# Row taps and group-norm moments placed at the slots in which ACT makes the silu

## The chip, the cores and the metric

The kernel runs on one core of a Trainium2 chip. The metric is the device time of one execution in microseconds. A core has five engines with a queue each: PE (TensorE, matmuls), DVE (VectorE), ACT (ScalarE), POOL (GpSimd) and SP (SyncE, which issues most of the transfers). An engine works through its own queue in order and waits for others by semaphores, so the time depends on where each instruction stands in its queue as much as on how many there are.

## The reference, cut to what matters

Four layers are applied to four images of 384 channels and 48 x 48 positions, each as `x = x + layer(groupnorm(x))`. Everything is float32.

```python
# layer 0: a selective state space model over the 2304 positions of an image
xin, z = split(norm(x) @ in_proj)
xin = silu(conv4(xin) + b)                       # 768 channels
dt, B, C = split(xin @ x_proj);  dt = softplus(dt @ dt_proj + b)
h[t] = exp(dt[t] * A) * h[t-1] + dt[t] * B[t] * xin[t]        # 768 channels x 16 states
y[t] = sum over states of h[t] * C[t]
out = layernorm(((y + xin * D) * silu(z)) @ out_proj)
# layer 1: 1x1 product, 8x8 patches filtered in the frequency domain, then
t = depthwise_conv3x3(t)                         # nine taps per channel
out = (gelu(t[:192]) * t[192:]) @ w_out
# layer 2: depthwise 11x11 convolution with kernels made from four points
# layer 3: four experts (384 -> 384 -> 384) weighted by a top-2 softmax gate
```

The group norm takes mean and variance of 12 channels over a whole image, so an image's layer can't begin before the moments of all its positions are known. For layer 0 these are moments of the input `x` itself.

## The kernel before, in words

**The scans.** Layer 0 sets the beat. An image is cut into five chunks of 460 or 464 positions. For each chunk there are 96 *slots*: 6 groups of 128 channels times 16 states, one state of one group per slot. There are 4 x 5 x 96 = 1920 slots, numbered through, and the number of the current one is kept in `place[0]`. In a slot `u` the function `scans` writes, in this order: background steps that begin on ACT; the scan of `u` on DVE (line 850); the other background steps; the product with C of `u` on DVE (line 870), or for the "slow" units one slot later on POOL (line 879); the decay `exp(dt * A)` of a later unit on ACT (line 826, three slots ahead in image 0, two ahead after it); the driving term of unit `u + 3` on POOL (line 837). After a scan and its product, ACT copies the last column to `carry` (line 864). PE sums the 16 states by transposing each result into PSUM (line 770).

**The background.** All other work is written as tasks: Python generators that yield an engine's name ahead of each step. A `Lane` holds a queue of tasks and in each slot moves each active task by at most one step, if the step's ring of buffers has room and its extra condition, the fourth entry of what is yielded, holds. A step on PE carries a weight, and the `Meter` admits no more of them into a slot when the sum is over a limit. Three lanes are served: `aux` with the rest of layer 0 (`plan` gives each task the slot of the chunk from which it may start), `one` with layers 1, 2 and the scores of the previous image, and `two` with its experts. The order of all instructions is thus fixed when the program is built. From slot 42 of images 1 to 3 the previous image's layers are put into `one` and `two`.

**The silu.** Once per chunk, `gates` takes the silu of the next chunk's `xc` and of this chunk's `zs`, 128 x 2760 elements each, on ACT (lines 693 and 696). Silu is in another table set than exp and ln, so a table load stands in front and one behind (line 548). It is due at slot 64 of a chunk and is written in slot 65.

**The moments of the next image.** `image_stats` loads half of 128 channels of the next image (1152 positions, three pieces of 384) into a buffer with the tag `on`, which the output of layer 0's projection also uses, lets six slots pass, and takes the moments of the three pieces on DVE (line 573), one piece per slot. It runs in the first three chunks of images 0 to 2, with the first half due at slot 43 and the second at 66.

**The taps.** `finish_strip` makes the nine taps of layer 1's 3 x 3 convolution for a strip of eight rows on DVE (lines 1272 and 1274), three channel groups in turn with one PSUM bank for the sum. A step takes three taps in two of four slots (`slow_slot`) and two in the others.

Of the kernel before, what the change touches and what calls it, by code (L numbers as in the profile page):

```python
# [133 lines left out]
def wait(slots):  # L134
    for _ in range(slots):
        yield ("pool",)
# [3 lines left out]
def tile_layers(ctx: ExitStack, tc: tile.TileContext, a: dict, out: bass.AP):  # L140
# [272 lines left out]
    with ExitStack() as first:  # L413
# [58 lines left out]
        with (  # L472
# [4 lines left out]
            for ct in range(CT):  # L477
                t = pp.tile([P, HW], F32, name=f"x0_{ct}")
# [62 lines left out]
        stats3 = [wp.tile([P, CT, len(BANDS), 6], F32, name=f"stats3_{b}") for b in range(2)]  # L541
        edges = [sum(BANDS[:k]) for k in range(len(BANDS) + 1)]

        ordered = [False]

        def table_back():

            ins = nc.scalar.preload_act_table_set("natural_log_exp_and_others")
            if not ordered[0]:
                tc.keep_in_program_order(ins)  # L550
# [2 lines left out]
            for _ in steps:  # L553
                pass

        def scans(wk, mm, ring, meter, place, lanes, begin):

# [6 lines left out]
            def image_stats(b, ct, h):  # L566
                t = wk.tile([P, TT * C], F32, name=f"xs0_{b}_{ct}_{h}", tag="on", bufs=1)
                half = HW // 2
                nc.sync.dma_start(t[:, :half], a["x"][b, bass.ts(ct, P), bass.ts(h, half)])
                yield from wait(6)  # L570
                for k in range(3):
                    yield ("dve",)
                    nc.vector.bn_stats(stats0[:, b % 2, ct, h, k, :], t[:, bass.ts(k, LB)])

            def image_norm(b):
# [112 lines left out]
            def gates(i, j):  # L688

                yield ("act",)  # L690
                if i is not None:
                    c, n = st[i], CHUNKS[G[i][1]]
                    nc.scalar.activation(c["xc"][:, :, :n], c["xc"][:, :, :n], AF.Silu)
                if j is not None:
                    c, n = st[j], CHUNKS[G[j][1]]
                    nc.scalar.activation(c["zs"][:, :, :n], c["zs"][:, :, :n], AF.Silu)
                table_back()
# [197 lines left out]
            def gate(i, m):  # L895
                (b, t), c = G[i], st[i]
                n = CHUNKS[t]
                w = n // TT
                yield ("pe", 0.45, (ring, 1))
                ps, r = ring.take(f"pyb{b}_{t}_{m}")  # L900
                for k in range(TT):
                    nc.tensor.transpose(
                        ps[:, bass.ts(k, w)], c["yt", m][:w, bass.ts(k, P)], ident[:w, :w]
                    )
                yield ("dve",)
                zm = c["zs"][:, m, :n]
                nc.vector.tensor_tensor(zm, ps[:, :n], zm, ALU.mult)
                ring.done(r)
# [75 lines left out]
            def plan(i, at):  # L984

                todo = []

                def put(q, name, make, *needs):
                    task = Task(make, [named[k] for k in needs if k in named], at + q)
                    named[name] = task  # L990
                    todo.append((q, task))

                more = i + 1 if i + 1 < len(G) else None
                if i:
                    for h in range(2):
                        put(6 + h, ("gate", i - 1, MT - 2 + h),
                            lambda h=h: gate(i - 1, MT - 2 + h))
                    for k in range(TT):
                        put(8 + 5 * k, ("out", i - 1, k), lambda k=k: out_proj(i - 1, k),
                            *[("gate", i - 1, m) for m in range(MT)])  # L1000
                    put(28, ("norm", i - 1), lambda: layer_norm(i - 1),
                        *[("out", i - 1, k) for k in range(TT)])
                    for ct in range(CT):
                        put(33 + 2 * ct, ("res", i - 1, ct), lambda ct=ct: residual(i - 1, ct),
                            ("norm", i - 1))
                if i < len(G):
                    b, t = G[i]
                    rest = [("res", i - 1, ct) for ct in range(CT)]
                    for j in range(MT):
                        put(30 + 4 * j, ("z", i, j), lambda j=j: project_z(i, j),  # L1010
                            ("out", i - 1, TT - 1), ("fold", b, 1))
                    for p in range(1, MT // 2):
                        put(PAIR * p - 12, ("steps", i, p), lambda p=p: steps(i, p))
                    for p in range(MT // 2):
                        put(PAIR * p + 14, ("skip", i, p), lambda p=p: skip(i, p))
                    done = [("z", i, j) for j in range(MT)]
                    if more is not None:
                        put(40, ("load", more), lambda: load(more), *rest)
                        for j in range(MT):
                            put(45 + 3 * j, ("x", more, j), lambda j=j: project(more, j),  # L1020
                                ("load", more), ("fold", G[more][0], 0))
                            done.append(("x", more, j))
                    put(64, ("silu", i), lambda: gates(more, i), *done)
                    if more is not None:
                        put(66, ("expand", more), lambda: expand(more), ("silu", i),
                            *[("steps", i, p) for p in range(MT // 2)])
                        put(82, ("steps", more, 0), lambda: steps(more, 0), ("expand", more))
                    for m, q in ((0, 67), (1, 69), (2, 74), (3, 76)):
                        put(q, ("gate", i, m), lambda m=m: gate(i, m), ("silu", i))
                    if b + 1 < NB:  # L1030
                        if t < CT:
                            put(43, ("stats", b, t, 0), lambda: image_stats(b + 1, t, 0), *rest)
                            put(66, ("stats", b, t, 1), lambda: image_stats(b + 1, t, 1),
                                ("stats", b, t, 0))
                        if t == CT:
                            put(48, ("mean", b + 1), lambda: image_norm(b + 1))
                            put(70, ("fold", b + 1, 0), lambda: fold(b + 1, 0),
                                ("mean", b + 1), *done)
                        if t == CT + 1:
                            put(54, ("fold", b + 1, 1), lambda: fold(b + 1, 1), *done[:MT])  # L1040
                aux.queue.extend(task for _, task in sorted(todo, key=lambda x: x[0]))
# [81 lines left out]

        def slow_slot():
            return place[0] % 4 < 2

        def later(b, ring, accr):

# [123 lines left out]
            def finish_strip(hb):  # L1252
# [7 lines left out]
                def taps(ct):  # L1260
                    yield ("dve", 0, (accr, 1))
                    acc, k = sums[ct] = accr.take(f"dw{b}_{hb}_{ct}")
                    v = acc[:, :LB].rearrange("p (h w) -> p h w", w=W)
                    room = 3 if slow_slot() else 2
                    for k in range(9):
                        if not room:
                            yield ("dve",)
                            room = 3 if slow_slot() else 2
                        room -= 1
                        src = d["pad", hb][:, ct, k // 3 : k // 3 + 8, k % 3 : k % 3 + W]  # L1270
                        if k == 0:
                            nc.vector.tensor_scalar_mul(v, src, w_dw[:, ct, 0:1])
                        else:
                            nc.vector.scalar_tensor_tensor(  # L1274
                                v, src, w_dw[:, ct, k : k + 1], v, ALU.mult, ALU.add
                            )
# [476 lines left out]

        rings = {}
        holder = [None]
        place = [0]

        def of_experts(pool, sizes):
            for tag, n in sizes.items():
# [16 lines left out]
        ring, accr = psum("mm", 3), psum("acc", 1)  # L1776
        meter = Meter(2.3, 2.0)
        one, two = Lane(8, meter), Lane(4, meter)
# [14 lines left out]
        with (  # L1793
            tc.tile_pool(name="l0", bufs=2) as wk,
            tc.tile_pool(name="l0p", bufs=2, space=PSUM) as mm,
        ):
            holder[0] = mm
            scans(wk, mm, ring, meter, place, [one, two], begin)
            held, two.queue = two.queue, []
            at = place[0]  # L1800
            while not all(ring.read):
                at += 1
                for act in (True, False):
                    two.step(act, at)
            two.queue = held
# [138 lines left out]
```

## Time and profile before

| | |
|---|---|
| median of three runs | 5437.34 us (5428.49 to 5438.78) |
| the profiled execution, its own time | 5425.31 us |
| its span, first to last instruction | 5423.4 us |
| mean granted TensorE clock | 0.913 |
| scan, line 850 | 1920 times, 1.16 to 1.18 us |
| decay, line 826 | 1920 times, 0.65 us |
| driving term, line 837 | 1920 times, 1.17 us |
| product with C on DVE, line 870 | 1035 times, 0.63 us |
| tap, line 1274 | 576 times, 0.61 us |
| moments of the next image, line 573 | 54 times, 0.53 us |
| silu, lines 693 and 696 | 20 each, 2.50 and 2.49 us |
| table load | 1.28 us |

The profile names an instruction by its engine, its line and its tiles, written as out<-in. A matmul of float32 stands twice in the trace, so a product of nine matmuls is 18 records. An instruction's recorded time runs a little into the next one's, so the distance of starts is often a better measure of what it costs than its own duration. Where an engine was idle, the profile gives the time and the instruction that ended it.

### The profile page before, as it was taken

What the parts mean: (1) busy time and instruction counts of PE and PEld (TensorE: products, weight loads), DVE (VectorE), ACT (ScalarE), POOL (GpSimd) and SP (SyncE); (2) the same over time, 40 slices, a digit from 0 to 9 for tenths busy, and PEclk for the clock granted to TensorE, in tenths of its full rate; (3) what the DMA queues carried; (4) which work ended last, traced back from release to release, by engine and by line L of the source; (5) the groups of instructions that cost most, each with busy time, mean ns of one, the idle gap of its engine ahead of it and who ended that gap; (6) DMA issues with size and microseconds to landing.
All of it is one profiled execution on the core that took longest, in us unless ns stands there. A gap on an engine that the chain in (4) does not pass through costs nothing. (4 is left out here: it accounts for less than half of the span.)

```text
span 5423.4 us, 81753 instructions
## 1 busy us (share of the span) xinstructions
PE 4666.9 (86%) x27796; PEld 3676.0 (68%) x27796; DVE 4053.8 (75%) x5581; ACT 2985.2 (55%) x6632; POOL 3365.2 (62%) x3020
## 2 busy tenths in 40 slices
PE   5677677687678988988789999988899999999899
PEld 4444454454347767665678887765678878889799
DVE  5999989889998788899887778899977674452200
ACT  3565565565558765655467655665566653334321
POOL 3878878876678788765667678775777673000000
PEclk8788788788789999999899999999999999999899
DMA  4445445454345555644566566554655554543200
GB/s 123 138 136 148 127 128 146 126 150 132 106 129 150 146 161 164 177 143 139 155 169 176 149 170 171 156 158 129 170 157 169 157 167 143 166 140 112 64 27 23
DMA packets 628391, 758.95 MB, mean 140 GB/s; under 512 B 58869, under 2 KB 622181, under 8 KB 627582
## 3 DMA queue, kind: packets, MB, share of 16 engines
q1 hardware_dynamic: 617668, 751.98, 48.2%
q8 instruction: 221, 3.62, 0.3%
q10 hardware_dynamic: 10298, 1.67, 0.2%
q14 instruction: 204, 1.67, 0.1%
HBM read 663.81 MB, written 89.65 MB: 139 GB/s over the span
## 5 line engine op out<-in xcount | busy, mean ns | idle before, releaser
L837 POOL TENSOR_TENSOR bu<-u,B 128x460 f32<-128x460 f32 (+1 forms) x1920 | 2227.5, 1170 | 778.2 <-DVE g L850 395.5
L826 ACT ACTIVATE da<-dt,a_neg 128x460 f32<-128x460 f32 (+1 forms) x1920 | 1242.8, 649 | 281.9 <-DVE g L870 185.4
L770 PE MATMUL y<-ident,g 128*115 128x128 f32 (+1 forms) x7680 | 1140.2, 297 | 274.1 <-DVE g L870 164.1
L770 PEld LDWEIGHTS y<-ident,g 128*115 128x115 f32 (+1 forms) x7680 | 1011.0, 187 | 502.3 <-DVE g L870 199.2
L879 POOL TENSOR_TENSOR g<-g,C 128x460 f32<-128x460 f32 (+1 forms) x885 | 1030.5, 1164 | 276.8 <-ACT carry L864 270.4
L850 DVE TENSOR_TENSOR_SCAN da<-da,carry,bu 128x460 f32<-128x460 f32 (+1 forms) x828 | 971.3, 1173 | 133.3 <-ACT da L826 94.7
L850 DVE TENSOR_TENSOR_SCAN g<-da,carry,bu 128x460 f32<-128x460 f32 (+1 forms) x708 | 819.7, 1167 | 83.5 <-ACT da L826 35.3
L870 DVE TENSOR_TENSOR g<-da,C 128x460 f32<-128x460 f32 (+1 forms) x1035 | 653.9, 632 | 91.7 <-PE y L770 31.5
L864 ACT COPY carry<-da 128x1 f32<-128x1 f32 x828 | 130.5, 158 | 824.3 <-DVE g L870 821.2
L1609 PE MATMUL pout<-hr,we 128*128 128x144 f32 x3456 | 483.6, 296 | 41.7 <-ACT hr L1625 31.7
L1609 PEld LDWEIGHTS pout<-hr,we 128*128 128x128 f32 x3456 | 455.4, 196 | 64.9 <-ACT hr L1625 42.6
L1609 PE MATMUL ph<-xe,we 128*128 128x144 f32 x3456 | 470.1, 291 | 13.4 <-DMA xe<-x3d 7.5
L1609 PEld LDWEIGHTS ph<-xe,we 128*128 128x128 f32 x3456 | 446.8, 194 | 30.6 <-issue 7.6
L1416 PE MATMUL pc<-band,row 128*128 128x162 f32 (+14 forms) x3456 | 458.8, 287 | 6.3 <-ACT row L1403 6.0
L1416 PEld LDWEIGHTS pc<-band,row 128*128 128x128 f32 x3456 | 446.2, 196 | 11.9 <-ACT row L1403 7.5
L1274 DVE SCALAR_TENSOR_TENSOR dw<-pad,w_dw,dw 128x384 f32<-128x384 f32 x576 | 347.6, 614 | 17.6 <-ACT pad L1249 6.7
L642 PE MATMUL pin<-xch,w_inx 128*128 128x463 f32 (+2 forms) x720 | 327.9, 595 | 34.7 <-DMA xch<-in_x 15.2
L921 PE MATMUL po<-w_out,zs 128*115 128x384 f32 (+1 forms) x960 | 341.5, 499 | 6.9 <-DVE dt L750 6.4
L1625 ACT ACTIVATE hr<-ph,nb 128x144 f32<-128x144 f32 x576 | 176.4, 377 | 305.2 <-PE ph L1609 303.6
L674 PE MATMUL pinz<-xch,w_inz 128*128 128x460 f32 (+1 forms) x720 | 316.8, 578 | 0.0
L1383 ACT ACTIVATE rep<-x,br,wr 128x192 f32<-128x192 f32 x576 | 274.3, 541 | 4.2 <-issue 4.2
L661 DVE SCALAR_TENSOR_TENSOR xc<-pin,conv_w,xc 128x460 f32<-128x460 f32 (+1 forms) x360 | 249.2, 692 | 30.9 <-ACT xc L655 19.2
(202 smaller groups left out, 5797.6 us busy)
## 6 DMA issues: line engine op xcount, KB each, us to landing
B<-bcd SPq DMA_DIRECT2D x768, 230.0 KB, 3.5
C<-bcd SPq DMA_DIRECT2D x768, 230.0 KB, 3.7
B<-bcd SPq DMA_DIRECT2D x192, 232.0 KB, 3.7
C<-bcd SPq DMA_DIRECT2D x192, 232.0 KB, 4.2
xe<-x3d SPq DMA_DIRECT2D x192, 216.0 KB, 2.8
ye<-y3d SPq DMA_DIRECT2D x144, 216.0 KB, 2.8
y3d<-ye SPq DMA_DIRECT2D x96, 216.0 KB, 2.2
xs<-x1d SPq DMA_DIRECT2D x24, 576.0 KB, 4.6
```

The source lines that it names most:

```text
L642: nc.tensor.matmul(ps[:, lo : halo + n], lhsT=w_inx[:, k, bass.ts(j, P)], rhs=c["x"][:, k, lo : halo + n], start=k == 0, stop=k == CT - 1,)
L674: nc.tensor.matmul(ps[:, :n], lhsT=w_inz[:, k, bass.ts(j, P)], rhs=c["x"][:, k, DCONV - 1 : DCONV - 1 + n], start=k == 0, stop=k == CT - 1,)
L770: nc.tensor.matmul(c["y", m][:w, bass.ts(k, P)], lhsT=src[:, bass.ts(k, w)], rhs=ident, is_transpose=True, start=c["terms", m] == 1 and k ...
L826: nc.scalar.activation(da[:, :n], c["dt", p][:, m % 2, :n], AF.Exp, scale=a_neg[:, m, s : s + 1])
L837: nc.gpsimd.tensor_mul(bu[:, :n], c["u", p][:, m % 2, :n], live["B", u // 2][:, :n])
L850: nc.vector.tensor_tensor_scan(here[:, :n], da[:, :n], bu[:, :n], last if t else nil[:, 0:1], ALU.mult, ALU.add,)
L870: nc.vector.tensor_mul(live["g", u][:, :n], live["h", u][:, :n], live["C", u // 2][:, :n])
L879: nc.gpsimd.tensor_mul(g[:, :n], g[:, :n], live["C", u // 2][:, :n])
L921: nc.tensor.matmul(ps[:w, :C], lhsT=c["zs"][:, m, bass.ts(k, w)], rhs=w_out0[:, m, :], start=m == 0, stop=m == MT - 1,)
L1274: nc.vector.scalar_tensor_tensor(v, src, w_dw[:, ct, k : k + 1], v, ALU.mult, ALU.add)
L1416: nc.tensor.matmul(d["acc2"][0][:, : BANDS[k] * W].rearrange("p (h w) -> p h w", w=W)[:, lo - edges[k] : hi - edges[k], xlo:xhi], lhsT=d[" ...
L1609: nc.tensor.matmul(ps[:, bass.ts(m, EB)], lhsT=w[:, k, bass.ts(m, P)], rhs=of[:, k, :], start=k == 0, stop=k == CT - 1,)
```

## The change

A function `gated` is true in the slot in which `gates` wrote its silus and in the next. The second half of `image_stats` waits until it is true and then takes its three moments in one slot; its load is due at slot 56 of the chunk instead of 66. A step of taps takes up to six while `gated` is true. `place`, so far handed to `scans`, is defined ahead of it. Nothing is added to or taken from the computation.

```diff
+        place = [0]
+        gated_at = [-9]
+
+        def gated():
+
+            return gated_at[0] <= place[0] <= gated_at[0] + 1
...
-        def scans(wk, mm, ring, meter, place, lanes, begin):
+        def scans(wk, mm, ring, meter, lanes, begin):
...
                 yield from wait(6)
+                if h:
+                    yield ("dve", 0, None, lambda: gated())
                 for k in range(3):
-                    yield ("dve",)
+                    if not h:
+                        yield ("dve",)
                     nc.vector.bn_stats(stats0[:, b % 2, ct, h, k, :], t[:, bass.ts(k, LB)])
...
                 yield ("act",)
+                gated_at[0] = place[0]
                 if i is not None:
...
-                            put(66, ("stats", b, t, 1), lambda: image_stats(b + 1, t, 1),
+                            put(56, ("stats", b, t, 1), lambda: image_stats(b + 1, t, 1),
                                 ("stats", b, t, 0))
...
+        def room_for_taps():
+            return 6 if gated() else 3 if slow_slot() else 2
+
...
-                    room = 3 if slow_slot() else 2
+                    room = room_for_taps()
                     for k in range(9):
                         if not room:
                             yield ("dve",)
-                            room = 3 if slow_slot() else 2
+                            room = room_for_taps()
```

More of the change, by code (lines that the diff above doesn't have):

```diff
@@ L1755, in tile_layers @@
         holder = [None]
-        place = [0]
         def of_experts(pool, sizes):
@@ L1797, in tile_layers @@
             holder[0] = mm
-            scans(wk, mm, ring, meter, place, [one, two], begin)
+            scans(wk, mm, ring, meter, [one, two], begin)
             held, two.queue = two.queue, []
```

## The prediction

> **What bounds the kernel now.** I read the shares by engine first, then who waited for whom, then the order of time around one silu, and last the busy time of stretches.
>
> ```profile
> PE 4666.9 (86%) x27796; PEld 3676.0 (68%) x27796; DVE 4053.8 (75%) x5581; ACT 2985.2 (55%) x6632; POOL 3365.2 (62%) x3020
> ```
> No engine bounds the whole. The 1920 scans (one per slot) run from 87 to 4525 us of the span, the rest of layers 1 to 3 after them. Busy time in stretches of 100 us has DVE at 88 to 96% and PE at 65 to 77% while image 0 is scanned, and PE at 90 to 100% where layers 2 and 3 run beside the scans. The chain that ended last is almost all PE, in the tail after 4525 us; the change leaves the order there as it was, so what it does to the scans shifts the end.
>
> Waits (microseconds in total, times, longest):
> ```profile
> POOL g L879 <- ACT carry L864: 270.4, 158, 8.2
> DVE da L850 <- ACT da L826: 107.3, 79, 8.1
> ```
> The silu slots make most of the second and part of the first. ACT around the first of them, in order of time (start, duration):
> ```profile
> 205.48 1.28 ACT L693 ACT_TABLE_LOAD   x1
> 206.77 2.50 ACT L693 ACTIVATE xc<-xc 128x2760 f32<-128x2760 f32 x1
> 209.18 2.49 ACT L696 ACTIVATE zs<-zs 128x2760 f32<-128x2760 f32 x1
> 211.68 1.28 ACT L548 ACT_TABLE_LOAD   x1
> ```
> ACT is shut for 7.5 us. DVE has three decays in hand, runs dry and waits:
> ```profile
> 208.22 1.17 DVE L850 TENSOR_TENSOR_SCAN g<-da,nil,bu 128x460 f32<-128x460 f32 x1
> 213.92 1.18 DVE L850 TENSOR_TENSOR_SCAN da<-da,nil,bu 128x460 f32<-128x460 f32 x1 [4.53 <-ACT carry L864]
> 216.92 0.64 DVE L907 TENSOR_TENSOR zs<-pyb,zs 128x460 f32<-128x460 f32 x1 [1.82 <-PE pyb L902]
> 223.28 1.17 DVE L850 TENSOR_TENSOR_SCAN da<-da,nil,bu 128x460 f32<-128x460 f32 x1
> 224.36 0.53 DVE L573 BATCH_NORM_STATS2 stats<-xs 128x6 f32<-128x384 f32 x1
> 224.81 0.62 DVE L870 TENSOR_TENSOR g<-da,C 128x460 f32<-128x460 f32 x1
> ```
> The 4.53 us are bubble, while three moments, the first at 224.36, stand in full slots soon after. In layer 1's stretches taps fill part of the hole already (silu slots 641, 1121, 1601):
> ```profile
> 1407.58 1.18 DVE L850 TENSOR_TENSOR_SCAN da<-da,carry,bu 128x460 f32<-128x460 f32 x1 [1.60 <-ACT carry L864]
> 2546.12 1.18 DVE L850 TENSOR_TENSOR_SCAN da<-da,carry,bu 128x460 f32<-128x460 f32 x1 [2.12 <-ACT da L826]
> 3747.91 1.18 DVE L850 TENSOR_TENSOR_SCAN da<-da,carry,bu 128x460 f32<-128x460 f32 x1 [4.75 <-ACT da L826]
> ```
>
> [...] the tiny carry copies behind the silus wait, and POOL's product behind a copy waits 7.04 us. [...] the silu starts 0.01 us after the load ends. [...] a moment is recorded with 0.53 us, but the product starts 0.45 us after it. I use such start-to-start times. [...]
>
> **The change, part by part.** The instructions are the same in number on every engine; only places move. I compared the two programs' orders, counting slots by scans. The silu slots are the same.
>
> *Second-half moments.* Nine groups of three (three chunks each before images 1 to 3) move from seven to nine slots after the silu into the silu slot, ahead of the bubble. Their load goes to SP's queue ten slots earlier (56 instead of 66). It needs the first half's moments, done five slots before, and the shared buffer "on" is next written at about slot 8 of the next chunk; neither waits. Inside the bubble a group takes 3 x 0.45 = 1.36 us of 4.53, so it is covered. Where it stood it cost less than 1.36: in a slot with a product on DVE the scan-to-product start distance is 1.26 us without a moment (1.08 to the moment), so a moment's removal saves 0.45 - 0.18 = 0.27; in a slot without, 0.45. Per group 0.27 + 0.45 + 0.27 = 1.0. The same slots of chunk 3 of image 0, which have no moments, take 1.8, 1.1, 1.8 us against 2.1, 1.5, 2.1: again 1.0.
> - Image 0 (silu slots 65, 161, 257): DVE bound, gaps of about 15 us in a chunk of 185: 3 x 1.0 = 3.0.
> - Slots 545, 737, 1025, 1217: the hole is 5.2 to 6.2 us, so cover is ample; but in the last three waits for PE follow within ten slots, so I keep half there: 1.0 + 3 x 0.5 = 2.5.
> - Slots 641 and 1121: counted with the taps.
>
> *Taps.* "Up to six" happens in two slots only. A tap's start-to-start time is 0.61 (three from 1400.82 to 1402.64).
> - 641: six taps instead of three, but two of the others stood in 642, ahead of the hole too. New work ahead of the wait: 1.36 + 0.61 = 2.0, hole 1.60. Gain 1.6, overflow 0.4 paid back as it is work taken from later.
> - 1602: six taps where two adds and moments (1.05) and no tap stood: 3.65 - 1.05 = 2.6 of 4.75. Gain 2.6. The product behind the six taps ends near 3745.8, before ACT is back (3747.07), so its carry copy isn't late.
> - 1121: layer 1 arrives three slots later, so five taps leave the front of the hole (1.82 + 1.16) and three moments plus an add and its moment come: 2.4 instead of 3.0. Loss 0.6.
>
> Sum at the silus: 3.0 + 2.5 + 1.6 + 2.6 - 0.6 = 9.1 us.
>
> *The shuffle behind it.* The taps' rooms set when layer 1's tasks end, and all later background work of images 1 and 2 moves: layer 2 up to 19 slots earlier, the experts up to 65, back in step from slot 1680. Work is conserved; it matters from where to where. Three stretches in the kernel before (slots 708 to 737, 833 to 960, 1368 to 1416), busy us of each engine:
> ```profile
> 1572.30:1639.70 67.40, 54.08 (x250) 34.45 (x248) 63.58 (x88) 38.86 (x90) 50.54 (x45) 0.94 0.52 154
> 1851.40:2128.30 276.90, 244.05 (x1477) 188.39 (x1476) 228.89 (x294) 175.28 (x326) 227.80 (x202) 0.91 0.54 160
> 3175.50:3293.20 117.70, 114.17 (x705) 87.58 (x704) 93.13 (x127) 69.61 (x119) 85.93 (x77) 0.97 0.59 163
> ```
> The third (PE 97%, DVE 79%) loses eight expert products of 9 matmuls, 2.37 us each, and gains two score blocks of about 2.7: -13.5 us of PE. The second (PE 88%) gains nine products and loses part of layer 2: +10.4. The first (PE 80%) gains +7, and the one between them (PE 95%) +3.6. Taken: relief -10 of 13.5 (DVE has 24.6 us free there), +4 of 10.4, +1 of 7, +2 of 3.6: -3. This is the unsure term: from -13 (relief in full, cost nil) to +21 (cost in full, no relief).
>
> Total 9.1 + 3 = 12. The profiled execution's own time is 5425.31 (span 5423.4, 1.9 around it), so a like one would be 5413. It lies 12 us below the median shown, 5437.34; I put the change to the median: **5425**.
>
> **Rivals.**
> *Nothing is kept after image 0.* Every DVE moment saved from slot 545 on is met by a PE or ACT wait. For it: waits for PE in 1025's and 1217's next slots. Against it: around 545, 641 and 1602 DVE runs without gaps. Saves 3: 5434.
> *The shuffle pays in full.* Experts leave a stretch with PE at 97% for stretches with holes. 9 + 13 = 22: 5415. Against it: the stretches that receive are not idle.
> *PE becomes the bound in 708 to 960 (slower).* All 7 + 3.6 + 10.4 = 21 us are paid there, and the relieved stretch runs no faster because DVE and ACT hold it. 21 - 9 = 12 slower: 5449. It decides once the unrelieved PE cost passes 9 us. For it: PE is at 95% in 737 to 833. Against it: 33 us of PE idleness in 833 to 960.
>
> **How the numbers follow.** Forecast 0.45 (own range 5419 to 5432), nothing kept 0.20, full shuffle 0.24, PE bound 0.11. The bound is 0.2%, about what a measurement of this kernel can tell from no change: 10.9 us, so below 5426.5 or above 5448.2. Faster: two thirds of the forecast (0.29) and the full shuffle, 0.53. Slower: 0.10, most of the last case. The rest, 0.37, is within. The range 5408 to 5442 leaves out the slower case and the far end of the full shuffle.
>
> **What would show it.** At 205 us three moments ahead of a gap of about 3.1 instead of 4.53, and 1.0 us less per chunk in image 0 for three chunks; at 1601 a gap near 2.1; at 641 none; slot 545 about 3 us earlier, slot 1920 about 12. Slots 1368 to 1416 should take about 108 instead of 117.7 us and 708 to 960 about 7 more. I am wrong if the chunks of image 0 keep their length (POOL or ACT sets the slots), or if 708 to 960 grows by over 15 us.

## The result, and the profile after

The changed kernel takes 5453.85 us, the median of seven runs (5443.51 to 5462.94). The kernel before, run beside it on the same chip, takes 5428.57 us (seven runs, 5416.32 to 5438.78). The ratio is 1.004 with an interval of 1.0025 to 1.0056: the change makes the kernel 25 us slower, where 12 us faster was forecast. The profiled execution took 5449.27 us (span 5447.1), against 5425.31 (5423.4) before, so its 24 us can be looked for in the traces. In the new kernel the lines are shifted by 10 to 14: the scan is line 861, the decay 837, the moments 583, the taps 1288, the products of layer 2's windows 1430.

The shares by engine of the kernel after:

```profile
PE 4672.0 (86%) x27796; PEld 3686.3 (68%) x27796; DVE 4057.3 (74%) x5581; ACT 2985.6 (55%) x6632; POOL 3364.9 (62%) x3020
```

The counts are those of before, and busy time grew by 5.1 us on PE and 3.5 on DVE. So most of the 24 us must be waiting: 18.6 us more on PE and 20.2 on DVE.

DVE in order of time around the first silu (start, duration, then in brackets the idle time before it and what ended it), kernel after:

```profile
205.81 1.45 DVE L583 BATCH_NORM_STATS2 stats<-xs 128x6 f32<-128x384 f32 x3
...
214.06 1.18 DVE L861 TENSOR_TENSOR_SCAN da<-da,nil,bu 128x460 f32<-128x460 f32 x1 [3.36 <-ACT carry L875]
```

The three moments stand ahead of the wait, which shrank from 4.53 to 3.36 us. Slots 71 to 75, where they stood before, fell from 7.5 to 6.5 us in each of the three chunks. This part does what was forecast (a gap of about 3.1).

The next table takes the distance of scans from both traces; the last column adds up what the kernel after lost since the start.

| slots | before, us | after, us | difference | sum so far |
|---|---|---|---|---|
| 0 to 641 | 1312.8 | 1308.7 | -4.1 | -4.1 |
| 641 to 684 | 110.9 | 112.1 | +1.2 | -2.9 |
| 684 to 960 | 617.6 | 647.5 | +29.9 | +27.0 |
| 960 to 1313 | 903.1 | 901.1 | -2.0 | +25.0 |
| 1313 to 1416 | 261.7 | 266.2 | +4.5 | +29.5 |
| 1416 to 1680 | 651.0 | 652.1 | +1.1 | +30.6 |
| 1680 to 1919 | 579.6 | 569.2 | -10.4 | +20.2 |
| tail | 899.6 | 903.0 | +3.4 | +23.6 |

All of the loss stands in one row, behind the first silu slot that takes six taps. Of the -10.4 near the end, 9.2 stand in slots 1800 to 1830, which take 69.9 to 79.4 us from one profile of this study to the next, with no relation to the edits; they count as chance. Slots 684 to 960 vary too: they take 617.6 to 624.0 us in the four kernels of this study whose background stands as before, and 643.5 to 647.5 in the six in which it is shifted as in the change. So the loss there is 20 to 30 us, and the 29.9 of this pair is its upper end.

Within slots 684 to 960 four stretches hold 26.9 of the 29.9 us. Busy time of each engine in the first three, kernel before (columns: window, its length, then PE, PEld, DVE, ACT, POOL with the number of records, granted clock of PE as a share of full speed, DMA share, GB/s):

```profile
1638.60:1661.49 22.89, 19.05 (x90) 14.68 (x91) 12.46 (x15) 20.79 (x38) 13.13 (x13) 0.78 0.39 121
1661.49:1706.06 44.57, 40.76 (x319) 38.85 (x318) 40.99 (x51) 38.32 (x95) 41.08 (x37) 0.94 0.54 155
2008.29:2080.73 72.44, 65.34 (x312) 37.04 (x310) 60.36 (x79) 46.95 (x71) 56.50 (x50) 0.95 0.62 190
```

The same slots (736 to 744, 744 to 768, 904 to 936), kernel after:

```profile
1639.29:1668.13 28.84, 18.61 (x104) 13.29 (x105) 15.15 (x20) 20.75 (x38) 13.16 (x13) 0.76 0.30 88
1668.13:1718.84 50.71, 47.10 (x360) 45.56 (x359) 40.17 (x48) 39.09 (x96) 43.03 (x39) 0.90 0.49 143
2020.78:2105.64 84.86, 75.71 (x430) 55.56 (x429) 63.30 (x88) 47.73 (x79) 57.26 (x50) 0.94 0.51 153
```

The second and third stretch grew by 6.1 and 12.4 us, and PE is busy 6.3 and 10.4 us longer in them, with 41 and 118 records more: work that now stands there seems to be paid for one to one or nearly so. In the second the granted clock is lower as well, 0.90 against 0.94; what that does comes up again below. The first grew by 6.0 us although PE is busy there no longer than before. The fourth stretch, 684 to 708, grew by 2.4.

What happens in the first of them, slots 736 to 744 around the silu of slot 737. PE, kernel after:

```profile
1640.70 1.59 PE L1430 MATMUL pc<-band,row 128*128 128x126 f32 x12 [2.44 <-ACT row L1417]
1650.21 1.50 PE L1430 MATMUL pc<-band,row 128*128 128x54 f32 x6 [7.92 <-ACT row L1417]
...
1653.48 3.62 PE L719 MATMUL pdbl<-xc,w_x 128*57 128x460 f32 x6
```

ACT at the same time, kernel after:

```profile
1643.47 2.50 ACT L704 ACTIVATE xc<-xc 128x2760 f32<-128x2760 f32 x1
1645.88 2.49 ACT L707 ACTIVATE zs<-zs 128x2760 f32<-128x2760 f32 x1
1648.39 1.28 ACT L555 ACT_TABLE_LOAD   x1
1649.68 0.48 ACT L1417 COPY row<-pr 128x384 f32<-128x384 f32 x1
```

A product of layer 2 needs a row that ACT copies out of PSUM. The copy stands behind both silus in ACT's queue, the product stands at the head of PE's, and everything behind it waits 7.92 us: the sums of the states and the projection `pdbl`, which doesn't need that row. PE doesn't go round it: `pdbl` starts at 1653.48, 3.27 us behind the product that waited (1650.21), though its operand was ready when the first silu ended, near 1646. In the kernel before, layer 2 stands at another of its products at this silu, whose row was copied ahead of the silus, and `pdbl` starts when the first silu ends. PE, kernel before:

```profile
1646.34 2.52 PE L708 MATMUL pdbl<-xc,w_x 128*57 128x460 f32 x6
```

### The profile page after: what moved, and what is told of

Read it like the earlier page. It is cut to its first block, busy times and chain, and to the rows that moved or that the text cites. A ratio compares the mean times of both kernels' runs of the same rounds, so it can differ in the third digit from the quotient of the medians.

```text
span 5447.1 us, 81746 instructions
## 1 busy us (share of the span) xinstructions
PE 4672.0 (86%) x27796; PEld 3686.3 (68%) x27796; DVE 4057.3 (74%) x5581; ACT 2985.6 (55%) x6632; POOL 3364.9 (62%) x3020
## 3 DMA queue, kind: packets, MB, share of 16 engines
q8 instruction: 221, 3.62, 0.3%
## 5 line engine op out<-in xcount | busy, mean ns | idle before, releaser
L1623 PE MATMUL pout<-hr,we 128*128 128x144 f32 x3456 | 490.0, 299 | 58.0 <-ACT hr L1639 48.3
L1623 PE MATMUL ph<-xe,we 128*128 128x144 f32 x3456 | 481.8, 296 | 27.2 <-DMA xe<-x3d 18.7
L671 DVE SCALAR_TENSOR_TENSOR xc<-pin,conv_w,xc 128x460 f32<-128x460 f32 (+1 forms) x360 | 249.3, 693 | 28.6 <-ACT xc L665 13.5
```

The source lines that it names most:

```text
L1623: nc.tensor.matmul(ps[:, bass.ts(m, EB)], lhsT=w[:, k, bass.ts(m, P)], rhs=of[:, k, :], start=k == 0, stop=k == CT - 1,)
```

## The experiments

After the two traces I held this theory: the moments are worth what was forecast; the taps lose, and not because of what they do in the silu slots but because they end layer 1's tasks earlier, so that all later background work stands in other slots. The rivals: the silu slots are overfilled, or one thing (an addition on DVE, a load, the experts, the held-up window) makes the whole loss and could be taken away. Diffs are against the kernel after unless said otherwise; times are medians, with the ratio to the kernel before of the same series and, in brackets, its 95% interval. There were three series, in which the kernel before took 5430.25 us (moments alone, taps alone, same steps, band), 5425.35 (first taps, window, experts, slot 1121) and 5427.17 us (the two at slot 664, weights).

### The two parts alone

Moments alone:

```diff
-            return 6 if gated() else 3 if slow_slot() else 2
+            return 3 if slow_slot() else 2
```

> Only the moments of the second halves move into the silu slots; taps keep three and two, so the background stands in the slots of the kernel before. If the shuffle of the background is what made the change slow, this is faster than before by 6 to 9 us (about 5421 against 5428), with slots 684 to 960 at the length of before. If work in a silu slot is itself harmful (late products, late carries), it is not faster, 5428 to 5440.

Measured: 5422.14 us, ratio 0.998 (0.997 to 0.999). In this series it is faster than both kernels; how firm that is comes up again at slot 1121.

Taps alone, with the moments put back as they were:

```diff
-                if h:
-                    yield ("dve", 0, None, lambda: gated())
                 for k in range(3):
-                    if not h:
-                        yield ("dve",)
+                    yield ("dve",)
...
-                            put(56, ("stats", b, t, 1), lambda: image_stats(b + 1, t, 1),
+                            put(66, ("stats", b, t, 1), lambda: image_stats(b + 1, t, 1),
```

> Only the taps take up to six in a silu slot; the moments stay where they were. The background moves exactly as in the changed kernel. Shuffle: slower than the changed kernel by what the moments save, some 30 us over before (about 5460). Silu slots overfilled: 641 and 1602 alone can't cost more than some microseconds, so near before, 5425 to 5435.

Measured: 5464.15 us, ratio 1.0066 (1.0049 to 1.0083). The moments gain 8 us and the taps lose 34; together they would lose 26, and the change loses 25. The parts add up, within a few us of noise, and the loss is the taps'.

The taps alone, and six only before slot 700, that is at silu 641:

```diff
-            return 6 if gated() else 3 if slow_slot() else 2
+            return 6 if gated() and place[0] < 700 else 3 if slow_slot() else 2
```

> Moments as before; six taps in slot 641 alone, three of them from slots 642 and 643. The background then moves as in the changed kernel up to slot 1440 and beyond. If these three taps set off the whole loss, the time is that of the taps alone, about 5460; if the six taps at 1602 have a part in it, it lies clearly below, 5430 to 5450.

Measured: 5461.88 us, 1.0064 (1.0045 to 1.0082). Three taps moved by a slot or two at one place make the whole loss of the taps.

### Is it the taps, or where the rest goes?

The taps taken early at the silu slots as in the change, but the number of steps kept, so that layer 1's tasks end in the slots of before:

```diff
+                    due = made = 0
+                    while due < 9:
+                        if due:
                             yield ("dve",)
...
+                        due = min(9, due + room_for_taps())
+                        upto = max(due, min(9, made + 6)) if gated() else due
+                        for k in range(made, upto):
```

with `room_for_taps` as in the moments alone.

> Moments as in the change; up to six taps in a silu slot too, but a channel group still gives up its later steps in the slots of before, so that nothing in the background moves (six taps stand one or two slots earlier). Shuffle: 8 to 11 us faster than before (about 5419), 1 to 3 us better than the moments alone. Overfilled silu slots: no better than the moments alone, and slots 641 and 1121 longer.

Measured: 5425.22 us, 1.0 (0.9988 to 1.0011). The loss is gone, so filling the silu slots isn't what loses. But the 8 to 11 us expected were not there. The taps add nothing to the moments at 641: slots 641 to 653 take 34.4 us here and 34.4 with the moments alone (35.0 before), since the three moments had filled all but 0.23 of the 1.60 us of idle time. At 1602 this kernel tests nothing: only six taps moved in it, at 641 and 1121, and slots 1601 to 1616 take 47.1 us (47.4 before). Nor does its time show the moments' own gain, though it has them.

The reverse test has six taps in slot 664, in which ACT makes no silu:

```diff
-            return 6 if gated() else 3 if slow_slot() else 2
+            return 6 if place[0] == 664 else 3 if slow_slot() else 2
```

> The moments alone, and six taps in slot 664, 23 slots away from any silu, with no silu slot taking more taps than before. Layer 2 and the experts of images 1 and 2 then stand in the slots that they have in the changed kernel. If the loss comes from where the background stands, this loses some 30 us against the moments alone: about 5452. If filling the silu slots with taps has a part in it, it stays near the moments alone, 5420 to 5430.

Measured: 5451.09 us, 1.0045 (1.0029 to 1.006), the time of the change. Its stretches are those of the change as well: 29.1, 48.3 and 85.8 us in slots 736 to 744, 744 to 768 and 904 to 936. The loss comes from where the background goes and not from the silu slot at which the taps stand. This pair of runs, the steps kept and slot 664, tells most of all.

The opposite direction, one tap instead of three in slot 664, so that the later work comes later:

```diff
-            return 6 if gated() else 3 if slow_slot() else 2
+            return 1 if place[0] == 664 else 3 if slow_slot() else 2
```

> The moments alone, with one tap instead of three in slot 664: layer 2 of image 0 moves up to 21 slots later and the experts 8 to 33 later, the other way than in the change. If the loss comes from work pulled ahead into a stretch that PE bounds, moving it back loses nothing or gains: 5405 to 5425. If the order of before fits the silus and the transfers better than its neighbours on both sides, it loses too: 5435 to 5455.

Measured: 5440.71 us, 1.0024 (1.0007 to 1.0041), in the range of the second expectation, but its reason isn't what the profile shows. In it the scans as a whole are as fast as with the moments alone (the last one starts at 4519.9 us against 4521.9), though slots 904 to 936 take 80.7 us here and 72.6 there. But an expert begins only behind the last scan: the next `xe` comes 15.6 us after it, against 3.0. The tail grows from 902.1 to 912.0 us. So what the profile shows of the loss is another one. It is not all: the profiled execution (5433.84) is one of the fastest of its six, and the other half of what the medians lose against the moments alone isn't located.

### Can one cause be taken away?

Three candidates were on the trace. The first was the addition of a band of layer 2 on DVE, which waits 7.78 us for PE in the silu slot:

```diff
-                    yield ("dve",)
+                    yield ("dve", 0, None, lambda: not gated())
```

> The changed kernel, with one condition more: layer 2's addition of a finished band is not let in at a silu slot. Two of them move, from slot 738 to 739 and from 833 to 835; all else stays. If the 7.78 us for which DVE waits at slot 738 for that band hold up the scans behind it, slots 736 to 744 lose 5 to 7 us of the 6 that they had gained, and the time is about 5447. If DVE would wait there for the decays anyway, the time stays at 5454.

Measured: 5455.61 us, 1.0044 (1.0029 to 1.0058); slots 736 to 744 still take 28.8 us. DVE, kernel with the band moved out:

```profile
1645.26 0.64 DVE L881 TENSOR_TENSOR g<-da,C 128x460 f32<-128x460 f32 x1 [8.76 <-PE y L781]
```

The addition is out of the way and the next instruction waits for PE instead. PE is what's late.

The second candidate was the window of layer 2 that holds PE. Held back for three slots:

```diff
-                yield ("pe", 1.68e-3 * (hi - lo) * 16 * NBC, (accr, 1) if first else None)
+                yield (
+                    "pe", 1.68e-3 * (hi - lo) * 16 * NBC, (accr, 1) if first else None,
+                    lambda: not 737 <= place[0] <= 739,
+                )
```

> The changed kernel, with layer 2's band matmuls not let in from slot 737 to 739, so that none of those whose rows ACT has yet to copy behind the silus stands on PE ahead of the silu's own products. Layer 2 is about ten slots later from there on. If PE's wait for such rows (7.92 us in the changed kernel) is what made slots 736 to 744 longer, they fall from 28.8 to about 23 us, and the time by 6 to 10. If the length of these slots has another cause, they stay at 28 to 29.

Measured: 5460.19 us, 1.0058 (1.004 to 1.0077). PE at slot 737, kernel with the window held:

```profile
1646.83 3.94 PE L719 MATMUL pdbl<-xc,w_x 128*57 128x460 f32 x6 [3.24 <-ACT xc L704]
```

`pdbl` now starts with the end of the first silu, and slots 736 to 744 fall from 28.8 to 24.2 us, 744 to 768 from 50.7 to 46.8. So the cause in slots 736 to 744 is shown: 4.7 of the 6.0 us go with the wait. In 744 to 768, where the kernel before takes 44.6, the 3.9 us came with a higher clock; kernel with the window held:

```profile
1664.24:1711.07 46.83, 42.47 (x351) 39.95 (x350) 39.70 (x47) 38.69 (x95) 42.50 (x39) 1.00 0.58 166
```

PE has 351 records in it instead of 360, and 319 before, at a clock of 1.00 instead of 0.90. And with six taps in slot 664 the same 360 records as in the kernel after took 48.3 us instead of 50.7, at a clock of 0.93. So a part of the 6.1 us that looked like work paid one to one was the clock. But the three slots move layer 2 once more, and the kernel loses elsewhere: against the change, 5.3 us in 960 to 1025, 7.4 in 1117 to 1313 and 10.1 in 1601 to 1680.

The third was the first expert of image 0, whose products stand in slots 904 to 936 of the kernel after and later in the kernel before. Held until slot 921:

```diff
-                yield ("pool", 0, None, lambda: rings["we"].free())
+                yield (
+                    "pool", 0, None,
+                    lambda: rings["we"].free() and (b or e or place[0] >= 921),
+                )
```

> The changed kernel, with the experts of image 0 not begun before slot 921. In slots 912 to 935 stand 5 expert products of 2.37 us, against 11 in the changed kernel and 1 in the one before; those left out stand from 960 on, 4 of them in 1368 to 1415. If expert work in a stretch that PE bounds is paid in full, slots 904 to 936 fall by 10 to 14 us from 84.9, slots 1368 to 1416 do not grow by more than 3, and the time is about 5445. If the stretch is long for another reason, it stays at 83 to 85.

Measured: 5469.86 us, 1.0076 (1.0058 to 1.0095), the slowest of all. Slots 904 to 936, kernel with the experts held:

```profile
2021.30:2100.00 78.70, 67.57 (x322) 47.35 (x321) 60.58 (x79) 45.45 (x69) 57.13 (x50) 0.85 0.49 147
```

Taking 8.1 us of PE out of the stretch makes it 6.2 shorter. That is half of its 12.4; 10 to 14 had been expected. PE has nearly the records of the kernel before again (322 against 312), but at a granted clock of 0.85 against 0.95 and with more idle time. And again it is paid elsewhere: slots 960 to 1025 grow by 9.9 us, 1368 to 1416 by 5.0, 1601 to 1680 by 10.5.

In the same stretch DVE waits for a load of C, kernel after:

```profile
2036.33 0.64 DVE L881 TENSOR_TENSOR g<-da,C 128x464 f32<-128x464 f32 x1 [6.24 <-DMA C<-bcd]
```

SP's queue ahead of it, kernel after:

```profile
2019.85 0.39 SPq L990 DMA_DIRECT2D x1d<-xch  x1
2025.61 0.38 SPq L634 DMA_DIRECT2D xch<-in_x  x1
2026.04 0.48 SPq L1580 DMA_DIRECT2D we<-in_L_w1T  x1
2026.57 0.49 SPq L1581 DMA_DIRECT2D we<-in_L_w2T  x1
...
2029.15 0.39 SPq L825 DMA_DIRECT2D C<-bcd  x1
```

The load of the input `xch` holds the queue for over 5 us (5.2 of them are its wait for the transfer `x1d<-xch`), and then the expert's weights go first. PE waits for that input as well, kernel after:

```profile
2030.33 4.10 PE L652 MATMUL pin<-xch,w_inx 128*128 128x460 f32 x6 [3.78 <-DMA xch<-in_x]
```

This wait isn't in the stretch of the kernel before, and with the experts held it is still 3.5 us. With the weights of this expert on ACT's queue:

```diff
-                nc.sync.dma_start(w[:, 0], per_channel(a["L3_w1T"][e]))
-                nc.sync.dma_start(w[:, 1], per_channel(a["L3_w2T"][e]))
+                queue = nc.sync if b or e else nc.scalar
+                queue.dma_start(w[:, 0], per_channel(a["L3_w1T"][e]))
+                queue.dma_start(w[:, 1], per_channel(a["L3_w2T"][e]))
```

> The changed kernel, with the first expert's two weight loads of image 0 issued from ACT's queue instead of SP's, where they stand behind a load that waits 5.8 us. If that pile of loads is why DVE waits 6.24 us for C at slot 910, the wait falls under 3 us and slots 904 to 928 from 58.8 to about 55; the time falls by no more than 4. If it is not, the wait stays over 5 us.

Measured: 5451.73 us, 1.0045 (1.0031 to 1.0059). The wait fell from 6.24 to 3.03 us, so the pile on SP's queue explains half of it, and the stretch stayed at 85.0 us. Half a wait of DVE taken away gained nothing; that PE sets the length here is read from its busy time (75.7 us in both). PE's own wait for `xch` stayed too, at 3.9 us.

### The one silu slot where moments lose

With the moments alone, slots 1117 to 1131 took 46.6 us instead of 43.9: at silu 1121 taps already fill the idle time. Against the moments alone, the group of that chunk is put back:

```diff
-                if h:
+                if h and (b, ct) != (3, 1):
                     yield ("dve", 0, None, lambda: gated())
                 for k in range(3):
-                    if not h:
+                    if not h or (b, ct) == (3, 1):
                         yield ("dve",)
...
-                            put(56, ("stats", b, t, 1), lambda: image_stats(b + 1, t, 1),
+                            put(66 if (b, t) == (2, 1) else 56, ("stats", b, t, 1), lambda: image_stats(b + 1, t, 1),
```

> The moments alone, but at slot 1121, where taps fill the hole already, they stay at slots 1128 to 1130 as before. If moments in a hole that is full push the product behind them late and cost more than they save, slots 1117 to 1131 fall back from 46.6 to 44 us, and the time is 2 to 4 us under the moments alone, 5417 to 5421. If that difference was chance, the time is that of the moments alone, 5422.

Measured: 5421.72 us, 0.9997 (0.9987 to 1.0007); slots 1117 to 1131 take 43.9 us again. Locally right, 2.7 us, but in the whole it can't be told from the moments alone (5422.14). How little one profile tells of such sums: in slots 0 to 1048 these two kernels have the same instructions in the same order, and their profiles reach slot 1048 6.7 us apart, in steps of 1 to 3 of both signs. For a few us only the medians of 14 runs count, and stretches that return the same in many profiles.

Even these medians leave the gain of the moments open. Against the kernel before of its own series the median of this kernel is 3.6 us lower, and its interval includes 1; so does that of the kernel with the steps kept (5.0 us lower). Of the three kernels that move the moments and leave the background in place, only the moments alone are faster clear of noise.

## Why the prediction was wrong, by its own steps

**Second-half moments: right.** Forecast were 1.0 us per group and 3.0 in image 0. Slots 71 to 75 of each of the three chunks fell by 0.96 us in each kernel that moves the moments, and in none that doesn't. The forecast missed two further gains of 2.5 us each in image 0 (slots 202 to 216 and 298 to 312, 28.9 and 28.8 us before, 26.4 and 26.4 after); they are in the last section. Of 545, 1025 and 1217 nothing can be told from noise: the ten slots from each take 26.2, 26.9 and 29.6 us before and 26.1, 26.6 and 28.6 after. By the medians of their series the moments alone gain 8 us, by the two other kernels 4 to 5; the 3.0 and the two times 2.5 in image 0 would be 8. Their profile gains 6.6 in slots 0 to 384 (743.0 to 736.4) and has lost it again at the end (span 5424.0 against 5423.4); what comes behind slot 384 is made of gains and losses of a few us, no larger than those between profiles of the same instructions. So the places are right and the total isn't settled.

**Taps: right at 1601, nothing at 641.** Slots 1601 to 1616 gained 3.7 us (2.6 forecast), the idle time there fell from 4.75 to 1.54 (2.1 forecast). At 641 the idle time went, as forecast, but the moments alone did that already, and the other taps are overflow: slots 641 to 653 took 1.9 us more. At 1121 a loss of 0.6 was forecast; with taps and moments moved the stretch gained 2.5 (43.9 to 41.4 us).

**The shuffle behind it: this step failed.** It was put at a gain of 3 us and costs about 30 by the medians (20 to 30 in slots 684 to 960). The stretches were right. The amounts were near for what was added (PE is busy 18.6 us longer in 708 to 960, 21 reckoned) and too high for the relief (6.6 us less in 1368 to 1416, 13.5 reckoned, with 97 records fewer but a clock of 0.94 against 0.97). And both sides were priced wrongly.

*What was added* to slots 708 to 960 was taken at 4 of 10.4, 1 of 7 and 2 of 3.6 us of PE work, 7 in all, since PE had idle time left. The stretch grew by 27.5. PE was idle on average, but not where the work went: 744 to 768 (PE busy 91% of it before) and 904 to 936 (90%) grew by about as much as PE's busy time in them, though a part of that is the clock and, in the second, other waits. The idle time that I counted on, 33 us in 833 to 960, was measured over 277 us, and 26 us of it fell outside 904 to 936. And 6 us came without any more PE work: a queue that stands still at silu 737, which no sum of work could show.

*What was taken away* from slots 1368 to 1416 was to bring 10 of 13.5 us. It brought 1.9. The distance of scans shows where it went:

| slots | before and moments alone | after | window held | experts held |
|---|---|---|---|---|
| 1368 to 1409 | 103.1 | 93.7 | 99.8 | 100.6 |
| 1409 to 1416 | 14.6 | 22.1 | 20.9 | 20.2 |

Up to slot 1409 the relief was 9.4 us, close to the 10 forecast. Slot 1409 is a silu slot. DVE around it, kernel before:

```profile
3273.97 0.16 DVE L609 TENSOR_SCALAR nwm<-pbias 128x6 f32<-128x6 f32 x1 [2.64 <-PE pbias L598]
3278.03 0.61 DVE L1641 TENSOR_TENSOR ye<-pout,ye 128x432 f32<-128x432 f32 x1 [3.90 <-PE pout L1609]
```

ACT at the same time, kernel before:

```profile
3273.33 2.50 ACT L693 ACTIVATE xc<-xc 128x2760 f32<-128x2760 f32 x1
3275.74 2.51 ACT L696 ACTIVATE zs<-zs 128x2784 f32<-128x2784 f32 x1
```

The silus ran in the shadow of DVE's waits for PE. Kernel after, DVE:

```profile
3304.10 1.19 DVE L861 TENSOR_TENSOR_SCAN da<-da,carry,bu 128x464 f32<-128x464 f32 x1 [2.26 <-ACT da L837]
...
3312.75 1.19 DVE L861 TENSOR_TENSOR_SCAN da<-da,carry,bu 128x464 f32<-128x464 f32 x1 [5.61 <-ACT da L837]
```

Kernel after, ACT:

```profile
3305.31 2.51 ACT L704 ACTIVATE xc<-xc 128x2760 f32<-128x2760 f32 x1
3307.72 2.50 ACT L707 ACTIVATE zs<-zs 128x2784 f32<-128x2784 f32 x1
```

Without the expert product of `ye` there is no such shadow, and DVE waits 7.87 us for ACT instead. Of the 9.4 us, 7.5 are given back in seven slots. This is read from the traces; no run moved that silu or that product alone. I had reckoned with DVE's 24.6 us of free time in this stretch, and not with the silu in it, though this prediction was about nothing else.

The absolute forecast, 5425, also started from a median of three runs, 5437.34; seven runs put the kernel before at 5428.57.

**The rival that came nearest** was *PE becomes the bound in 708 to 960*, at 5449 us and a chance of 0.11. Its place is right, its 21 us paid in full are close to the 18.5 by which the two dense stretches grew, though not all of that is work, and its relieved stretch that runs no faster is nearly right too: 1.9 us (it had named DVE and ACT as what holds it; the trace has ACT). It missed the 6 us of the standing queue. The sign that the prediction named, over 15 us of growth in 708 to 960, is there. It was given too little weight because PE's share was read over stretches of 70 to 280 us.

**What stays open.** That the background's new places make the loss is shown by six taps in slot 664 and by the steps kept. In 736 to 744 the mechanism is shown by the held window, and in 904 to 936 half of the growth by the held experts; of the 6.1 us in 744 to 768 some 2 to 4 go with the clock rather than with the work (an estimate, from the 48.3 us with six taps in slot 664 and the 46.8 with the window held against 50.7), and neither was tried apart. The other half in 904 to 936 is not tied to a cause by a run: PE's late input and the lower clock are the candidates on the trace. Nor are 5.5 us in the rest of 684 to 960. Whether there is an order of the background better than that of before was tried only in single places: the shifts to earlier and to later lost, and none of the four changes to single places (band, window, experts, weights) came back to the time before.

## What to carry to other kernels

In a program whose order is fixed when it is built, a step that ends one slot sooner moves all that is queued behind it: count what arrives where, and ask for each arrival which queue it can stop, before counting what the step itself gains. Read an engine's spare time in stretches as short as the work that moves in; and ask of a wait that goes away which other wait lay in its shadow, because only the difference of the two is gained. When both parts of a change are separable, run them apart: here the moments alone, at 0.998 of the kernel before in their series, were faster than both kernels, and the taps alone were slower than both.

## What the runs showed of the hardware

PE's granted clock drops to 0.50 for some us at a time, and at the same place it drops in one kernel and not in another. PE in image 0, kernel before:

```profile
480.99 4.05 PE L921 MATMUL po<-w_out,zs 128*115 128x384 f32 x6
...
485.49 2.10 PE L921 MATMUL po<-w_out,zs 128*115 128x384 f32 x6
```

A product of the same size takes 4.05 us and then 2.10. The granted clock (the column after POOL's), kernel before:

```profile
475.00:480.00 5.00, 1.58 (x13) 1.37 (x13) 4.86 (x8) 3.82 (x9) 4.37 (x5) 0.84 0.41 112
480.00:485.00 5.00, 5.00 (x11) 3.06 (x12) 4.82 (x6) 2.35 (x6) 4.35 (x5) 0.50 0.49 149
```

After 5 us in which PE was busy for 1.58 (its longest idle stretch in them took 2.98 us), the clock is 0.50 for the next five, while PE has work without a gap. It is 0.86 in the sixth and 1.00 in the seventh. The longest idle stretch alone doesn't foretell this drop: 2.98 us were followed by it here, and 2.97 us at the same place of the kernel with the moments alone were not:

```profile
480.00:485.00 5.00, 5.00 (x23) 3.28 (x24) 4.82 (x7) 2.45 (x7) 4.34 (x5) 1.00 0.49 149
```

There the product takes 2.10 us, and two waits of DVE behind it in the kernel before, 0.79 us for PE and 1.17 us for ACT, are gone. This fits the 2.5 us that slots 202 to 216 and 298 to 312 gain in every kernel that moves the moments: 26.3 or 26.4 us in all of those, 27.9 to 29.0 in the three that don't. Why the shift of the moments makes the drop go away was not tried by itself.

A drop also falls on the queue that stood still. From 1648 to 1656 us of the kernel after, at the end of the 7.92 us wait at silu 737 and behind it, the clock is 0.50 to 0.57, and six records of `pdbl` take 3.62 us where they took 2.52 before, just when they are late. The drop itself isn't new: in the kernel before the clock is 0.50 to 0.55 from 1640 to 1646 us, ahead of `pdbl`, and the mean over slots 736 to 744 is 0.78 there and 0.76 here.
